# A transformer pair in one core: matrix products issued in four column strips behind the attention outputs, a new clock for transfers, and a newly searched order

## The chip, the core and the metric

The kernel runs on one core of a Trainium2 chip. The metric is the device time of one execution in microseconds. Before the change the median of three runs is 1472.46 us (1472.16 to 1474.3).

## What is computed

Two transformer blocks in sequence on `x` of shape (32, 128, 256), all in float32, with 16 heads of 16 and a hidden layer of 1024. Each block has self-attention, cross-attention to `ctx_1024`, and a feed-forward part. Cut to what matters:

```
# block 1; mod = silu(cond) @ ada_w + ada_b, split into 6
xm1 = ln(x) * (1 + scale_sa) + shift_sa
x = x + gate_sa * (attn(xm1 @ qkv_w + qkv_b) @ sa_proj_w + sa_proj_b)
x = x + attn_masked(ln(x) @ q_w + q_b, ctx @ kv_w + kv_b) @ ca_proj_w + ca_proj_b
xm3 = ln(x) * (1 + scale_ff) + shift_ff
x = x + gate_ff * (gelu(xm3 @ fc1_w + fc1_b) @ fc2_w + fc2_b)
# block 2: the same shape with adaptive norms, rope on q and k, other weights, no gates
x = x + attn(rope(adaln1(x) @ qkv_w.T)) @ sa_out_w.T
x = x + attn(rope(adaln2(x) @ q_w.T), rope(ctx @ k_w.T), ctx @ v_w.T) @ ca_out_w.T
x = x + gelu(adaln3(x) @ ffn_w1.T + ffn_b1) @ ffn_w2.T + ffn_b2
```

## The kernel before, in words

The batch of 32 is cut into 16 groups of two sequences (256 tokens). Each group passes both blocks, so there are 32 group passes; eight streams of groups are under way at once, and their steps are interleaved so that every engine has work of some stream.

**The matrix engine's three ways of working.** A float32 matmul of the program shows as two records in the profile, each with its own weights load; a transpose shows as one.

- *Full*: the products of 128 x 128 weights with 256 moving columns (`rows_T` L604, `values` L616, `project` L844), the transposes of the normed tile (`transposed` L565) and of the score maxima (L754).
- *Rows*: the scores (L729). Four heads at a time use 32 of the 128 rows each, `scores` is one PSUM tile of four banks, and a batch needs two such groups of 16 matmuls: one to find the maxima, one with the maxima subtracted from the queries.
- *Columns*: the attention outputs (L775). Four heads at a time use 32 of the 128 columns each, 16 matmuls to a group, into the PSUM tile `small`.

There are 128 batches (32 passes, two attentions, two sequences), so 256 rows groups and 128 columns groups. Products go to three PSUM tiles of one bank, `products0` to `products2`.

**One attention and what follows it.** Scores; VectorE takes the maxima (L741); TensorE turns them (L754); VectorE subtracts them from the queries (L758, tile `qa`); scores again; ScalarE takes the exponential (L767); the outputs (L775), whose sums of exponentials come along as extra columns; ScalarE copies them (L781). Then `over_sums` (L786 to L810): a DMA gathers the sums (`few`, L793), another the outputs (L795), VectorE takes the reciprocal (L798), a DMA writes it to DRAM (`inv`, L801), two DMAs bring it back spread (L806), and VectorE multiplies (L809). Only then may `project` (L844) start, after which `normed_T` runs: statistics on VectorE (L540, L541), the power on GpSimd (L547), the normed tile (L553), and the transposes (L565).

**What sets the order.** The instructions of each engine stand in a fixed order that a planner writes when the program is built. Every step is a generator that yields when it can start, on which engine, which buffers it needs and a rank. `Clock` (L41) keeps a planned time for each engine and buffer; its costs are constants in the code (`use`, L57; `dma`, L70; `load`, L75). `Tasks.run` (L143) takes step after step, the one with the earliest planned start, and breaks near ties by rank. `ORDER` (L35) holds one number for each 40 us of planned time; it sets how far a later step may be preferred and shuffles the ranks. The clock knows that TensorE loses time when it goes from one way of working to another (`TURN`, L46), and it counts buffers: one `sc` (`scores`), one `at` (`small`), three `mm` (`products`). All DMAs are issued by SyncE, in the order planned. In `dma`, a transfer takes a fixed time from its issue, whatever else is under way.

**Weights.** Each weight tile is loaded twice, first for block 1, later for block 2. `Weight.used` (L216) counts uses; at the last one of block 1 it issues the reload at once, inside the product's own step (`second`, L266), and the planner reckons 3.0 us for each.

Of the kernel before, what the change touches and what calls it, by code (L numbers as in the profile page):

```python
# [17 lines left out]
P = 128  # L18
# [16 lines left out]
ORDER = (  # L35
    6622, 0, 91896, 0, 27754, 24892, 69964, 0, 30721, 66120, 0, 41605, 0, 69433, 0, 43084, 27437, 27178, 72830,
    16201, 38328, 98324, 37276, 0, 13032, 79752, 41486, 59529, 18013, 48897, 61204, 13263, 51033, 0, 0, 0, 0
)


class Clock:  # L41
# [71 lines left out]
def when(t):  # L113
    return t() if callable(t) else t
# [93 lines left out]
class Weight:  # L208
# [6 lines left out]

    def used(self):  # L216
        self.left -= 1
        if self.left == 0:
            self.there[1] = self.load()


@with_exitstack
def two_blocks(ctx: ExitStack, tc: tile.TileContext, a: dict, out: bass.AP):
# [24 lines left out]
    p_a = pool("p_a", 1)  # L248
    p_s = pool("p_s", NS + 2)

    def mm(shape):
# [356 lines left out]

    def values(wm, hd, w, col, src, t):

        yield after(wm, w, t), "pe", "mm", 1.5
        slot = clock.take("mm")
        ps = mms[slot].rearrange("p (b d) -> p b d", d=D)
        for b in range(GB):
            for k in range(KC):
                nc.tensor.matmul(ps[:, b, :], lhsT=src[:, k, b * S:(b + 1) * S],  # L616
                                 rhs=w.t[:, k, col:col + D], start=(k == 0), stop=(k == KC - 1))
        w.used()
        t = clock.use("pe", 1.72)
        there = Event()  # L620

        def evict():
            yield t, "act", "", 2
            nc.scalar.copy(hd.v[:, :, :, 0], ps)  # L624
            clock.give("mm", slot, there.add(clock.use("act", 0.6)))

        tasks.spawn(evict(), wm)
        return there


    def paired(hd, wm, w, src, t):
# [30 lines left out]
        def move():  # L662
            yield here, "sp", "", 1
            nc.sync.dma_start(out=hd.k[0:P:2, :, :], in_=st[1:P:2, :, :])
            clock.give("st", at, there.add(clock.dma(2.7)))

# [25 lines left out]
    def turned(to, wm, w, col, src, t):  # L692
# [7 lines left out]
        def move():  # L700
            yield t, "dve", "", 1
            for b in range(GB):
                one = slice(b * S, (b + 1) * S)
                nc.vector.tensor_tensor(st[:, :, :, one], ps[:, :, one].unsqueeze(2).to_broadcast([P, 2, 2, S]), rope,  # L704
                                        ALU.mult)
            end = clock.use("dve", 1.25)
            clock.give("mm", slot, end)
            yield end, "pool", "", 1
            nc.gpsimd.tensor_tensor(st[:, 0], st[:, 0], st[:, 1], ALU.add)  # L709
            yield clock.use("pool", 1.27), "sp", "", 4  # L710
            for e in range(2):
                nc.sync.dma_start(out=to[2 * e:P:4, :, :], in_=st[:, 0, e, :])
                end = clock.dma(2.3)
            clock.give("st", at, there.add(end))
# [4 lines left out]
    def attention(wm, hd, masked, t, t_v, name, done):  # L719
# [13 lines left out]
        def batch(b):  # L733
# [14 lines left out]
            clock.give("sc", slot, t_top)  # L748
            yield (lambda: max(t_top, when(second[b - 1]) if b else 0.0)), "pe", "at qa" if ou else "at qa ou", 0.5
            at, less = clock.take("at"), clock.take("qa")  # L750
            if not ou:
                ou.append(clock.take("ou"))
            ps = ats[at][:, 0:S]
            nc.tensor.transpose(ps, top.rearrange("p r i -> p (r i)"), ident)  # L754
# [4 lines left out]
            end = clock.use("dve", 0.7)  # L759
            clock.give("at", at, end)  # L760
            yield end, "pe", "sc pt", 0
# [7 lines left out]
            clock.give("sc", slot, end)  # L769
            yield (lambda: max(end, when(t_v))), "pe", "at", 1  # L770
            at = clock.take("at")
            for c in range(C):
                for r in range(R):
                    i = (R * c + r) * HD
                    nc.tensor.matmul(ats[at][32 * r:32 * r + 32, c * S:(c + 1) * S],  # L775
                                     lhsT=v[:, b, i:i + HD, :].rearrange("p d t -> p (d t)"),
# [3 lines left out]
            yield end, "act", "", 1  # L780
            nc.scalar.copy(ous[ou[0]][:, :, cut], ats[at].rearrange("p (c s) -> p c s", s=S))  # L781
            end = clock.use("act", 0.6)
            clock.give("at", at, end)
            copied.add(end)

        def over_sums():  # L786
# [6 lines left out]
            nc.sync.dma_start(out=few, in_=o[1:P:8, :, :])  # L793
            at = clock.dma(2.1)
            nc.sync.dma_start(out=wm.xt, in_=o[0:P:2, :, :])  # L795
# [5 lines left out]
            nc.sync.dma_start(out=inv.rearrange("r (t w) -> (r t) w", w=w), in_=few)  # L801
            yield clock.dma(1.6), "sp", "", 1
            by = o[:, 0:KC, :]
            for c in range(2):
                half = inv[:, c * KC * GT:(c + 1) * KC * GT]
                nc.sync.dma_start(out=by[c:P:2, :, :], in_=half.unsqueeze(1).to_broadcast([n, 4, KC * GT]))  # L806
                at = clock.dma(2.5)
            yield at, "dve", "", 1.5
# [10 lines left out]
    def project(wm, x, lhs, n, w, ready, bias, gate, name):  # L819
# [18 lines left out]
        for b in range(GB):  # L838
# [4 lines left out]
            for k in range(n):  # L843
                nc.tensor.matmul(ps[:, b, :], lhsT=lhs(k, b), rhs=w.t[:, k, :], start=(k == 0), stop=(k == n - 1))  # L844
            t = clock.use("pe", 0.43 * n)
        w.used()
        yield t, "dve", "", 1
# [40 lines left out]
    def load_gate(wm, which, g):  # L888
# [3 lines left out]
        nc.sync.dma_start(out=t, in_=gates[which][g * GB:(g + 1) * GB, :].partition_broadcast(P))  # L892
        clock.dma(3.6)
        return y

    def mask_row(hd, src, g):
        yield landed("masks"), "sp", "", 1
        row = src.rearrange("b s -> (b s)")[g * GT:(g + 1) * GT].unsqueeze(0).unsqueeze(0)
        nc.sync.dma_start(out=hd.k[MASK:P:32, :, :], in_=row.to_broadcast([R, C, GT]))
        return clock.dma(2.5)  # L900

    class Context:
# [5 lines left out]
        def fetch(self, wm):  # L908
# [3 lines left out]
            load_ctx(self.slot, self.g)  # L912
            self.there.add(clock.dma(3.0))

# [68 lines left out]
    def stream(wm, mine, loaded):  # L983

        while loaded:
# [13 lines left out]
            def next_x(i):  # L999
                load_x(xs[i], a["x"] if then < NG else middle, then % NG)  # L1000
                return xs[i], clock.dma(2.9)

# [11 lines left out]
            nc.sync.dma_start(out=to[g * GB:(g + 1) * GB].rearrange("b s d -> s b d"), in_=x)  # L1014
            end = clock.dma(2.2)
            if first:
# [99 lines left out]
```

## Time and profile before

| | |
|---|---|
| median of the runs | 1472.46 us (1472.16 to 1474.3) |
| time of the profiled execution | 1467.35 us |
| its span, first to last instruction | 1465.5 us |
| TensorE busy (matmul) | 1433.2 us, 98% |
| TensorE weights loads | 1183.2 us, 81% |
| VectorE, ScalarE, GpSimd busy | 883.9, 700.6, 356.3 us (60%, 48%, 24%) |
| main DMA queue | 117.98 MB, 25.8% of 16 engines' span |
| granted TensorE clock, mean | 0.997 |

The profile is of one execution. The busy time of the matmul row is the union of records that overlap, with ends that are modelled, so it cannot be read as work done at full rate; the distance from one record's start to the next one's start can. The profiled execution took 5.1 us less than the median of the runs (1472.46 - 1467.35).

### The profile page before, as it was taken

What the parts mean: (1) busy time and instruction counts of PE and PEld (TensorE: products, weight loads), DVE (VectorE), ACT (ScalarE), POOL (GpSimd) and SP (SyncE); (2) the same over time, 40 slices, a digit from 0 to 9 for tenths busy, and PEclk for the clock granted to TensorE, in tenths of its full rate; (3) what the DMA queues carried; (4) which work ended last, traced back from release to release, by engine and by line L of the source; (5) the groups of instructions that cost most, each with busy time, mean ns of one, the idle gap of its engine ahead of it and who ended that gap; (6) DMA issues with size and microseconds to landing.
All of it is one profiled execution on the core that took longest, in us unless ns stands there. A gap on an engine that the chain in (4) does not pass through costs nothing.

```text
span 1465.5 us, 39524 instructions
## 1 busy us (share of the span) xinstructions
PE 1433.2 (98%) x17016; PEld 1183.2 (81%) x17016; DVE 883.9 (60%) x1546; ACT 700.6 (48%) x1120; POOL 356.3 (24%) x498
## 2 busy tenths in 40 slices
PE   8999999999999999999999999999999999999998
PEld 7887888887788778888887888888787888787887
DVE  6766545546564475457575676675866655865642
ACT  6444554464554545535534444444444444544452
POOL 3222223222232312332232221220222211211211
PEclk9999999999999999999999999999999999999999
DMA  6343221313223223323212331221313111221210
GB/s 228 117 128 88 83 73 50 88 63 116 71 65 86 79 89 84 90 86 121 82 49 91 114 125 46 85 66 50 111 57 104 41 55 59 76 78 56 69 48 22
DMA packets 107360, 120.52 MB, mean 82 GB/s; under 512 B 11632, under 2 KB 82992, under 8 KB 107184
## 3 DMA queue, kind: packets, MB, share of 16 engines
q1 hardware_dynamic: 107184, 117.98, 25.8%
q8 instruction: 134, 2.20, 0.6%
q14 instruction: 42, 0.34, 0.1%
HBM read 54.92 MB, written 12.68 MB: 46 GB/s over the span
## 4 chain that ended last, share of the span: by engine, by line
PE 75%; DMA 8%; DVE 8%; issue 3%; POOL 2%; SPq 2%; ACT 2%; DVEq 0%; ACTq 0%; POOLq 0%
PE products L604 24%; PE products L844 20%; PE scores L729 15%; PE small L775 7%; PE products L616 5%; PE products L565 3%; DVE top L741 2%; DMA ou<-inv_d 1%; PE small L754 1%; DMA inv_d<-few_d 1%; DMA few_d<-ou 1%; DVE st L704 1%; ACT exp L767 1%; SPq L806 1%; DMA ou<-inv_a 1%
## 5 line engine op out<-in xcount | busy, mean ns | idle before, releaser
L741 DVE TENSOR_REDUCE top<-scores 128x8 f32<-128x1024 f32 x256 | 300.2, 1214 | 59.7 <-PE scores L729 44.4
L767 ACT ACTIVATE exp<-scores 128x1024 f32<-128x1024 f32 x256 | 248.3, 1023 | 174.4 <-PE scores L729 173.4
L604 PE MATMUL products<-xt,w_ffn_w 128*128 128x256 f32 x1024 | 238.5, 384 | 0.3 <-ACT ht L873 0.2
L844 PE MATMUL products<-w_ffn_w,ht 128*128 128x256 f32 x1024 | 231.9, 381 | 0.0
L604 PEld LDWEIGHTS products<-xt,w_ffn_w 128*128 128x128 f32 x1024 | 189.3, 190 | 31.3 <-issue 1.8
L844 PEld LDWEIGHTS products<-w_ffn_w,ht 128*128 128x128 f32 x1024 | 191.8, 190 | 27.5 <-issue 0.8
L781 ACT COPY ou<-small 128x512 f32<-128x512 f32 x128 | 75.5, 590 | 210.5 <-PE small L775 209.9
L873 ACT ACTIVATE ht<-products,cols 128x256 f32<-128x256 f32 x256 | 116.4, 473 | 116.9 <-PE products L604 115.4
L729 PEld LDWEIGHTS scores<-qa,keys 32*128 32x128 f32 x4096 | 126.6, 187 | 44.7 <-issue 22.7
L709 POOL TENSOR_TENSOR st<-st 128x512 f32<-128x512 f32 x64 | 82.4, 1288 | 301.6 <-DVE st L704 295.3
L729 PEld LDWEIGHTS scores<-keys,queries 32*128 32x128 f32 x4096 | 126.0, 186 | 36.4 <-issue 21.2
L729 PE MATMUL scores<-qa,keys 32*128 32x128 f32 x4096 | 151.0, 284 | 3.4 <-DVE top L741 2.7
L729 PE MATMUL scores<-keys,queries 32*128 32x128 f32 x4096 | 150.4, 283 | 3.9 <-DVE top L741 1.8
L775 PE MATMUL small<-exp,values 128*32 128x128 f32 x4096 | 139.1, 276 | 0.1
L604 PE MATMUL products<-xt,w_qkv_w 128*128 128x256 f32 x512 | 125.0, 389 | 0.8 <-DVE xt L585 0.8
L775 PEld LDWEIGHTS small<-exp,values 128*32 128x32 f32 x4096 | 104.3, 109 | 24.2 <-issue 11.6
L758 DVE TENSOR_TENSOR qa<-queries,small 128x512 f32<-128x512 f32 x128 | 86.3, 674 | 55.7 <-PE small L754 50.9
L849 DVE TENSOR_TENSOR x<-products,x 128x512 f32<-128x512 f32 x64 | 43.9, 686 | 121.2 <-PE products L844 103.2
L604 PEld LDWEIGHTS products<-xt,w_qkv_w 128*128 128x128 f32 x512 | 94.3, 192 | 16.6 <-issue 2.4
L624 ACT COPY values<-products 128x512 f32<-128x512 f32 x64 | 40.0, 626 | 122.1 <-PE products L616 120.0
L809 DVE TENSOR_TENSOR xt<-xt,ou 128x512 f32<-128x512 f32 x64 | 48.2, 754 | 81.5 <-DMA ou<-inv_b 26.2
L704 DVE TENSOR_TENSOR st<-products,rope 128x512 f32<-128x512 f32 x128 | 81.8, 680 | 21.8 <-PE products L604 14.8
(111 smaller groups left out, 1734.5 us busy)
## 6 DMA issues: line engine op xcount, KB each, us to landing
xt<-ou SPq DMA_DIRECT2D x64, 256.0 KB
keys<-st SPq DMA_DIRECT2D x96, 128.0 KB
queries<-st SPq DMA_DIRECT2D x96, 128.0 KB
cxt<-in_ctx SPq DMA_DIRECT2D x32, 256.0 KB
x<-in_x SPq DMA_DIRECT2D x16, 256.0 KB
keys<-st SPq DMA_DIRECT2D x16, 256.0 KB
y<-gate_dram_sa SPq DMA_DIRECT2D x16, 256.0 KB
ou<-inv_a SPq DMA_DIRECT2D x32, 128.0 KB
```

Source lines behind the costliest of these rows:

```text
L604: nc.tensor.matmul(ps[:, c, :], lhsT=w.t[:, k, at:at + P], rhs=src[:, k, :], start=(k == 0), stop=(k == KC - 1))
L616: nc.tensor.matmul(ps[:, b, :], lhsT=src[:, k, b * S:(b + 1) * S], rhs=w.t[:, k, col:col + D], start=(k == 0), stop=(k == KC - 1))
L704: nc.vector.tensor_tensor(st[:, :, :, one], ps[:, :, one].unsqueeze(2).to_broadcast([P, 2, 2, S]), rope, ALU.mult)
L709: nc.gpsimd.tensor_tensor(st[:, 0], st[:, 0], st[:, 1], ALU.add)
L729: nc.tensor.matmul(sc[:, r, c * S:(c + 1) * S], lhsT=lhs(slice(32 * r, 32 * r + 32), c), rhs=rhs(slice(32 * r, 32 * r + 32), c), start=Tru ...
L741: nc.vector.tensor_reduce(top[:, r:r + 2, TOP:TOP + 2 * C:2], scs[slot][:, r:r + 2, :].rearrange("p r (c s) -> p r c s", s=S), AX.X, ALU.max)
L758: nc.vector.tensor_tensor(qa, q[:, :, cut], ps.unsqueeze(1).to_broadcast([P, C, S]), ALU.subtract)
L767: nc.scalar.activation(exps[pt][r // 2], scs[slot][:, r:r + 2, :], AF.Exp, scale=SCALE)
L775: nc.tensor.matmul(ats[at][32 * r:32 * r + 32, c * S:(c + 1) * S], lhsT=v[:, b, i:i + HD, :].rearrange("p d t -> p (d t)"), rhs=exps[pt][r ...
L781: nc.scalar.copy(ous[ou[0]][:, :, cut], ats[at].rearrange("p (c s) -> p c s", s=S))
L844: nc.tensor.matmul(ps[:, b, :], lhsT=lhs(k, b), rhs=w.t[:, k, :], start=(k == 0), stop=(k == n - 1))
L873: nc.scalar.activation(ht[f // (FC // 2)][:, f % (FC // 2), :], ps[:, 0, :], AF.Gelu, bias=b1[:, f:f + 1])
```

## The change

Five things are edited; the kernel's mathematics and tiles stay, apart from PSUM.

1. **Products behind outputs in columns.** A new function `multiply` issues a product either as one matmul of 128 weight columns or, if the planned way of working is "columns" at that point, as four matmuls of 32 weight columns, each to its own 32 partitions of the same PSUM tile. `rows_T`, `values` and `project` call it, and tell the clock that they take "any" way: columns if the engine is in columns, full otherwise.
2. **PSUM.** The tile `small` is gone, a fourth `products` tile takes its bank, and the turned maxima and the attention outputs take a `products` tile.
3. **The clock of transfers.** In `dma` a transfer's planned end comes behind that of the transfer before it (`moved`); the durations given to it are lowered by 0.1 to 0.5 us (one stays), the reloads' aside.
4. **Reloads.** A weight's reload is a step of its own on SyncE with rank 3, planned for the end of the last use. The two halves of the key and value weights are two steps. Their planned time depends on the size.
5. **Order.** `ORDER` holds new numbers, so that every engine's sequence is another one.

The diff, cut to its core:

```diff
 ORDER = (
-    6622, 0, 91896, 0, 27754, 24892, ...
+    71372, 36752, 0, 0, 71454, 91697, ...
 )
-        many = {"sc": 1, "at": 1, "mm": 3, "pt": 2, "set": NA, "qa": 2, "ou": 3, "st": 2, "ht": 1,
+        many = {"sc": 1, "mm": 4, "pt": 2, "set": NA, "qa": 2, "ou": 3, "st": 2, "ht": 1,
                 "y": 3, "cx": 3, "x": NS + 1}
+        self.moved = 0.0
...
         if engine == "pe":
+            if way == "any":
+                way = "columns" if self.way == "columns" else "full"
             took = took * self.PACE + (self.TURN[self.way] if way != self.way else 0.0)
             self.way = way
...
     def dma(self, took):
         start = max(self.now, self.free["sp"])
         self.free["sp"] = start + 0.64
-        return start + took
+        self.moved = max(self.moved, start + 0.9) + max(0.1, took - 1.4)
+        return self.moved + 0.5
 
     def load(self, kb):
...
         self.landed = max(self.landed, start + 1.5) + kb / 200.0
+        self.moved = self.landed
         return self.landed + 0.7
...
-    def used(self):
+    def used(self, at):
         self.left -= 1
         if self.left == 0:
-            self.there[1] = self.load()
+            self.load(self, at)
...
-    ats = [psum.tile([P, C * S], F32, name="small")]
-    mms = [psum.tile([P, 2 * GT], F32, name=f"products{i}") for i in range(3)]
+    mms = [psum.tile([P, 2 * GT], F32, name=f"products{i}") for i in range(4)]
...
+    def multiply(to, lhs, rhs, start=True, stop=True):
+        if clock.way == "columns":
+            for j in range(0, P, 32):
+                nc.tensor.matmul(to[j:j + 32], lhsT=lhs[:, j:j + 32], rhs=rhs, start=start, stop=stop)
+        else:
+            nc.tensor.matmul(to, lhsT=lhs, rhs=rhs, start=start, stop=stop)
...
-        def second():
-            n = cols // len(names)
-            for i, name in enumerate(names):
-                load(t[:, :, i * n:(i + 1) * n], f"L1_xcond_{name}")
-                end = clock.dma(3.0)
-            return end
+        def second(w, at):
+            def loading():
+                n = cols // len(names)
+                for i, name in enumerate(names):
+                    yield at, "sp", "", 3
+                    load(t[:, :, i * n:(i + 1) * n], f"L1_xcond_{name}")
+                    w.there[1] = clock.dma(2.0 + 3e-6 * 4 * rows * n)
+                    if i < len(names) - 1:
+                        w.there[1] = NEVER
+            tasks.spawn(loading(), Setup())
...
-                nc.tensor.matmul(ps[:, c, :], lhsT=w.t[:, k, at:at + P], rhs=src[:, k, :],
-                                 start=(k == 0), stop=(k == KC - 1))
-        w.used()
-        return slot, ps, clock.use("pe", 0.86 * n)
+                multiply(ps[:, c, :], w.t[:, k, at:at + P], src[:, k, :], k == 0, k == KC - 1)
+        end = clock.use("pe", 0.86 * n, "any")
+        w.used(end)
+        return slot, ps, end
...
-            yield (lambda: max(end, when(t_v))), "pe", "at", 1
-            at = clock.take("at")
+            yield (lambda: max(end, when(t_v))), "pe", "mm", 1
+            at = clock.take("mm")
```

More of the change, by code (lines that the diff above doesn't have):

```diff
@@ L35 @@
 ORDER = (
[L36 to L37 removed]
+    71372, 36752, 0, 0, 71454, 91697, 0, 94157, 73524, 26634, 81926, 67541, 0, 14443, 0, 59342, 0, 88828, 0,
+    12337, 30536, 2421, 29624, 8901, 84470, 22357, 96881, 43920, 51881, 25816, 98785, 9044, 8412, 0, 96954, 9117,
+    0
 )
@@ L615, in values @@
             for k in range(KC):
[L616 to L619, printed above, removed]
+                multiply(ps[:, b, :], src[:, k, b * S:(b + 1) * S], w.t[:, k, col:col + D], k == 0, k == KC - 1)
+        t = clock.use("pe", 1.72, "any")
+        w.used(t)
         there = Event()
@@ L664, in move @@
             nc.sync.dma_start(out=hd.k[0:P:2, :, :], in_=st[1:P:2, :, :])
-            clock.give("st", at, there.add(clock.dma(2.7)))
+            clock.give("st", at, there.add(clock.dma(2.3)))
         tasks.spawn(move(), wm)
@@ L712, in move @@
                 nc.sync.dma_start(out=to[2 * e:P:4, :, :], in_=st[:, 0, e, :])
-                end = clock.dma(2.3)
+                end = clock.dma(2.0)
             clock.give("st", at, there.add(end))
@@ L748, in batch @@
             clock.give("sc", slot, t_top)
-            yield (lambda: max(t_top, when(second[b - 1]) if b else 0.0)), "pe", "at qa" if ou else "at qa ou", 0.5
-            at, less = clock.take("at"), clock.take("qa")
+            yield (lambda: max(t_top, when(second[b - 1]) if b else 0.0)), "pe", "mm qa" if ou else "mm qa ou", 0.5
+            at, less = clock.take("mm"), clock.take("qa")
             if not ou:
                 ou.append(clock.take("ou"))
-            ps = ats[at][:, 0:S]
+            ps = mms[at][:, 0:S]
             nc.tensor.transpose(ps, top.rearrange("p r i -> p (r i)"), ident)
@@ L759, in batch @@
             end = clock.use("dve", 0.7)
-            clock.give("at", at, end)
+            clock.give("mm", at, end)
             yield end, "pe", "sc pt", 0
@@ L774, in batch @@
                     i = (R * c + r) * HD
-                    nc.tensor.matmul(ats[at][32 * r:32 * r + 32, c * S:(c + 1) * S],
+                    nc.tensor.matmul(mms[at][32 * r:32 * r + 32, c * S:(c + 1) * S],
                                      lhsT=v[:, b, i:i + HD, :].rearrange("p d t -> p (d t)"),
@@ L780, in batch @@
             yield end, "act", "", 1
-            nc.scalar.copy(ous[ou[0]][:, :, cut], ats[at].rearrange("p (c s) -> p c s", s=S))
+            nc.scalar.copy(ous[ou[0]][:, :, cut], mms[at].rearrange("p (c s) -> p c s", s=S))
             end = clock.use("act", 0.6)
-            clock.give("at", at, end)
+            clock.give("mm", at, end)
             copied.add(end)
@@ L793, in over_sums @@
             nc.sync.dma_start(out=few, in_=o[1:P:8, :, :])
-            at = clock.dma(2.1)
+            at = clock.dma(2.0)
             nc.sync.dma_start(out=wm.xt, in_=o[0:P:2, :, :])
@@ L801, in over_sums @@
             nc.sync.dma_start(out=inv.rearrange("r (t w) -> (r t) w", w=w), in_=few)
-            yield clock.dma(1.6), "sp", "", 1
+            yield clock.dma(1.5), "sp", "", 1
             by = o[:, 0:KC, :]
@@ L806, in over_sums @@
                 nc.sync.dma_start(out=by[c:P:2, :, :], in_=half.unsqueeze(1).to_broadcast([n, 4, KC * GT]))
-                at = clock.dma(2.5)
+                at = clock.dma(2.3)
             yield at, "dve", "", 1.5
@@ L843, in project @@
             for k in range(n):
-                nc.tensor.matmul(ps[:, b, :], lhsT=lhs(k, b), rhs=w.t[:, k, :], start=(k == 0), stop=(k == n - 1))
-            t = clock.use("pe", 0.43 * n)
-        w.used()
+                multiply(ps[:, b, :], lhs(k, b), w.t[:, k, :], k == 0, k == n - 1)
+            t = clock.use("pe", 0.43 * n, "any")
+        w.used(t)
         yield t, "dve", "", 1
@@ L892, in load_gate @@
         nc.sync.dma_start(out=t, in_=gates[which][g * GB:(g + 1) * GB, :].partition_broadcast(P))
-        clock.dma(3.6)
+        clock.dma(3.4)
         return y
@@ L899, in mask_row @@
         nc.sync.dma_start(out=hd.k[MASK:P:32, :, :], in_=row.to_broadcast([R, C, GT]))
-        return clock.dma(2.5)
+        return clock.dma(2.0)
     class Context:
@@ L912, in fetch @@
             load_ctx(self.slot, self.g)
-            self.there.add(clock.dma(3.0))
+            self.there.add(clock.dma(2.8))
     def attended(wm, at, x, masked, t, t_v, w, bias, gate, eps, mod, g, name, then, cx=None):
@@ L1000, in next_x @@
                 load_x(xs[i], a["x"] if then < NG else middle, then % NG)
-                return xs[i], clock.dma(2.9)
+                return xs[i], clock.dma(2.7)
             if then is not None and clock.slot("x") < NEVER:
@@ L1014, in stream @@
             nc.sync.dma_start(out=to[g * GB:(g + 1) * GB].rearrange("b s d -> s b d"), in_=x)
-            end = clock.dma(2.2)
+            end = clock.dma(2.1)
             if first:
```

## The prediction

> **What bounds the kernel now.** I read the page's busy shares first, then the chain that ended last, then TensorE's own waits, then a stretch of its timeline.
>
> ```profile
> span 1465.5 us, 39524 instructions
> ...
> PE 1433.2 (98%) x17016; PEld 1183.2 (81%) x17016; DVE 883.9 (60%) x1546; ACT 700.6 (48%) x1120; POOL 356.3 (24%) x498
> ...
> PE 75%; DMA 8%; DVE 8%; issue 3%; POOL 2%; SPq 2%; ACT 2%; DVEq 0%; ACTq 0%; POOLq 0%
> ```
>
> TensorE is the bound; no other engine passes 60%. A quarter of the chain runs over others, but eight streams fill those times, as TensorE's own waits show (us in total, times, longest):
>
> ```profile
> PE products L565 <- DVE y L553: 8.0, 7, 3.3
> PE products L844 <- DVE xt L809: 5.9, 8, 1.3
> PE scores L729 <- DVE top L741: 4.6, 7, 1.8
> ...
> PE scores L729 <- DMA keys<-st: 1.2, 1, 1.2
> ```
>
> All waits in that list sum to 27 us. So either TensorE's own work gets shorter, or little happens. How long the work is, the timeline of TensorE tells, read from start to start (ends overlap):
>
> ```profile
> 737.79 1.08 PE L775 MATMUL small<-exp,values 128*32 128x128 f32 x32
> 738.80 3.72 PE L844 MATMUL products<-w_ffn_w,ht 128*128 128x256 f32 x16
> 742.45 1.08 PE L775 MATMUL small<-exp,values 128*32 128x128 f32 x32
> 743.46 1.17 PE L729 MATMUL scores<-keys,queries 32*128 32x128 f32 x32
> 744.57 0.66 PE L565 MATMUL products<-ident,y 128*128 128x128 f32 x4
> 745.06 3.62 PE L844 MATMUL products<-w_ffn_w,ht 128*128 128x256 f32 x16
> 748.51 0.27 PE L754 MATMUL small<-ident,top 128*128 128x128 f32 x1
> 748.72 1.17 PE L729 MATMUL scores<-keys,queries 32*128 32x128 f32 x32
> ```
>
> Sixteen product records that stay among full ones take 748.51 - 745.06 = 3.45 us, 0.216 each. The same sixteen between two columns groups take 742.45 - 738.80 = 3.65: 0.2 us more for two changes of the way of working. Over all records, the medians of start-to-start times give the prices: leaving full costs 0.093 us (0.309 against 0.216); entering full costs 0.104 with a product first (its first record takes 0.320) and 0.056 with a transpose first (0.165 against 0.109). A columns group takes 1.01 us, eight rounds of 0.109 and 0.139 for coming and going. A rows group takes 1.104.
>
> **The change, part by part.** Products in columns, and the new order around them, are one sum. I counted the stretches of one way of working in the instruction order of both programs:
>
> - stretches in full: 272 before (180 begin with a product, 88 with a transpose, 4 with a small modulation), 238 after (111, 124, 3);
> - stretches in columns: 129 before, 115 after, of which 72 hold products besides outputs;
> - stretches in rows: 256 in both, so they cancel.
>
> Leaving full: 34 fewer x 0.093 = 3.2 us. Entering full: 69 fewer with a product x 0.104 = 7.2, 36 more with a transpose x 0.056 = 2.0, net 5.2. Columns: 14 fewer x 0.139 = 1.9. Sum **10.3 us**, all on TensorE, hence on the path. As a check, the same prices and every record of the order sum to 1411.1 us before and 1400.9 after; 1465.5 - 1411.1 = 54.4 us of the span before are then true waits, start and tail.
>
> The price of a product in columns: 458 of 2048 products become four matmuls each (the order has 1832 of 32 columns by 256), 916 rounds counting both records. No row before shows four column strips with 256 moving columns. The nearest are the outputs' rows (count, busy us and mean ns of one, idle):
>
> ```profile
> L775 PEld LDWEIGHTS small<-exp,values 128*32 128x32 f32 x4096 | 104.3, 109 | 24.2 <-issue 11.6 <-ACT exp L767 1.1 <-ACT ou L781 0.7
> L775 PE MATMUL small<-exp,values 128*32 128x128 f32 x4096 | 139.1, 276 | 0.1
> ```
>
> A weights load is 0.109 us, yet four loads and four matmuls of 128 columns pass in each 0.109: the loads lie fully beside the streaming. The Trainium skill speaks against this (TensorE: Matmul & The Clock Gate, "The mechanism"): a weights load overlaps a running matmul only when it goes to other rows of the array. Strips of columns share all rows, so by the rule every round would wait 0.109 for its loads: 916 x 0.109 = +100 us. By the row (and by the full products, which load for 0.190 beside 0.216 of streaming) nothing waits: 256 moving columns give twice the cover of 128 and the round takes the same 0.216 as a full matmul: 0 us. I take 0. Below nothing isn't possible, since the streaming rate is the same. If a little of the cover is lost, the nearest number is what a columns group pays on its first round beyond the later ones, 0.024 us: x 916 = 22 us. Both passes of an output add to the same place in PSUM, round after round, without a gap, so accumulating over k shouldn't cost either.
>
> The fourth product tile in place of `small`: TensorE's weights loads waited 3.6 and 0.7 us in all for the copies out of `small` (L781), and a shared pool can shorten that or spread it to products; I take 0, bounds -4 to +4. The steps on VectorE and ScalarE that read it are the same in number and size; one more pair of table loads on ScalarE (65 to 67, 1.28 us each) lies in an engine at 48%.
>
> The reloads: eight DMAs, at nearly the same places of SyncE's queue (246th to 369th row before, 241st to 367th after). Before, SyncE stood 3.0 us before a reload for the product that last used the tile, with the attention's sums and keys queued behind; TensorE waited for no weights. Gain 0 to 3, and if one is late, a megabyte at the page's early 228 GB/s is about 5 us once. I take 0.
>
> The clock of transfers moves no transfer by itself; it leaves more room before the steps that wait for one. In the chain the same step takes from 1.98 to 3.28 us (`few`) and 2.53 to 3.55 (`ou` from `inv`), where the old clock has 2.1 and 2.5. What room can win is bounded by what TensorE waits behind DMAs: 5.9 us at L844 for the multiply of L809, about 4.6 more at its weights loads, 1.2 for keys: up to 12 us.
>
> Against it stands the new order, which is tighter elsewhere. Between two uses of the one `scores` tile, the exponential needs some 2.4 us (two of 1.02 and the hops). In PE work at the prices above, the old order leaves less in 8 places, 2.0 us short in all; the new one in 11 places, 7.9 us short (four of them in the first 110 us). From project to transposes the shortest gaps are 4.0, 4.0 and 4.2 us against 4.7, 4.8 and 4.7. Together some +8 us of new waits against up to -12 of removed ones. I let them cancel: the 54.4 us stay.
>
> Sum: span 1465.5 - 10.3 = 1455.2, profiled execution 1457; the median of the runs lies 5.1 above, **1462.2 us** (-0.7%).
>
> **Rivals.**
> - *The waits shrink* (chance 0.20). The 12 us behind DMAs go and the tight places cost little because they fall together with waits that stand there anyway: 1462.2 - 12 = 1450. For it: the spread of the transfers' times. Against: TensorE waits longest for VectorE, which no clock of transfers mends.
> - *Column products are slower* (0.12), the case on the other side. One mechanism: in the 72 mixed stretches each round pays part of its four loads. At 0.024 us a round it is 1462.2 + 22 = **1484**; by the skill's rule 1562. It decides from 10.3/916 = 0.011 us a round. Against it: the outputs' rounds of 0.109 without loss.
> - *The waits grow* (0.20): the tight places cost their 8 us, again as much behind them as other streams come late, and nothing is won at the DMAs: 1462.2 + 16 = 1478; half of that gives 1470.
> - *The change doesn't do what it says*: the order of the changed program shows the strips and the fewer stretches, so only their price is open; no chance of its own.
>
> **How the numbers follow.** The forecast's case has 0.48. Within 0.2% (1469.5 to 1475.4, about what a measurement of this kernel can tell from no change) lies half of the growing waits. Faster: 0.48 + 0.20 + 0.04 (the mildest growth) = 0.72. Same: 0.11. Slower: 0.12 + 0.05 = 0.17. The range reaches from 1448, just past the shrinking waits, to 1477 for most of the growing ones; the dear strips are left out. The likeliest case's own range is 1456 to 1469.
>
> **What would show it.** Right: sixteen product records of 32 columns by 256 between two columns groups follow at 0.216 a round, four records a round; no 0.32 first record after an output; TensorE's records sum to about 1401 and the rest of the span stays near 54. Wrong if the mean round of the strips is above 0.227, or if that rest moves by over 10 us; then the waits at `scores`, L565 and the multiply ahead of project tell which.

## The result, and the profile after

The changed kernel takes **1463.71 us** (median of 6 runs, 1459.99 to 1465.63) against 1472.95 us for the kernel before beside it (6 runs, 1472.16 to 1474.3): a ratio of 0.9934, 95% interval 0.9918 to 0.995. The forecast was 1462.2. The profiled execution took 1462.32 us, 1.4 us below the median; its mean granted TensorE clock was 0.994, where before's was 0.997.

The page of the kernel after, its span, its busy row and the shares of the chain:

```profile
span 1460.5 us, 45118 instructions
...
PE 1425.4 (98%) x19764; PEld 1136.3 (78%) x19764; DVE 889.2 (61%) x1538; ACT 707.5 (48%) x1130; POOL 357.2 (24%) x498
...
PE 83%; DVE 6%; DMA 5%; ACT 2%; POOL 2%; issue 1%; SPq 1%; DVEq 0%; ACTq 0%; POOLq 0%
```

There are 2748 more matmul records and 7.8 us less matmul busy time: the records have become smaller, and the stretches fewer. TensorE's share of the chain has gone from 75% to 83%, the transfers' from 8% to 5%.

The timeline of TensorE in the kernel after (start, duration, line, operation, output and inputs, tile, count) shows what a product in columns costs:

```profile
429.86 3.64 PE L262 MATMUL products<-w_ffn_w,ht 128*32 128x256 f32 x64
433.43 1.17 PE L749 MATMUL scores<-qa,keys 32*128 32x128 f32 x32
434.53 3.72 PE L264 MATMUL products<-w_ffn_w,ht 128*128 128x256 f32 x16
438.09 0.27 PE L774 MATMUL products<-ident,top 128*128 128x128 f32 x1
...
748.05 1.08 PE L795 MATMUL products<-exp,values 128*32 128x128 f32 x32
748.95 1.91 PE L262 MATMUL products<-w_qkv_w,xt 128*32 128x256 f32 x32
750.79 1.17 PE L749 MATMUL scores<-qa,keys 32*128 32x128 f32 x32
```

Thirty-two strips are eight rounds of four. From the strips' first start to the scores behind them they take 750.79 - 748.95 = 1.84 us: eight rounds of 0.216 and the 0.11 that leaving the columns costs anyway. The sixteen rounds at 429.86 take 3.57, again 0.216 each. The outputs ahead of them take 748.95 - 748.05 = 0.90 instead of 1.01, because the engine stays in columns. The sixteen full records at 434.53 behind a scores group take 3.56: sixteen of 0.216 and 0.104 for entering full. So a round of strips costs what a full record costs, although its four loads share all rows of the array with the matmul that runs. The rule of the Trainium skill that the prediction weighed (TensorE: Matmul & The Clock Gate, "The mechanism") does not hold here as it was read; by it, as an estimate, the 1.84 us would have been 8 x (0.216 + 0.109) + 0.11, about 2.7. The same section of the Trainium skill also lets a load go ahead into a background weight buffer; that would fit, but no run here shows how the loads are hidden.

What remains are TensorE's waits. The list for the kernel after (engine, line, the one waited for: us in total, times, longest):

```profile
PE products L586 <- DVE y L574: 6.7, 10, 2.4
PE scores L749 <- ACT exp L787: 6.7, 9, 1.8
PE products L264 <- DVE xt L829: 3.7, 6, 1.7
PE products L774 <- DVE top L766: 3.4, 2, 2.9
PE scores L749 <- DVE top L761: 2.7, 4, 1.0
PE products L262 <- DVE xt L829: 2.2, 2, 1.8
```

The line L829 (L809 before) multiplies the outputs by the inverted sums, which come back by a chain of small transfers. TensorE's waits for it were 5.9 us before and 3.7 + 2.2 = 5.9 after. A clock meant to leave more room for transfers won nothing there. The waits for the last step of the maxima (L766, from 1.6 us) and for the exponential (L787, from 0.4) have grown.

To tell work from waits I split every start-to-start time of TensorE into two parts: what the record and its change of way cost at the prices of the prediction, and the excess. The excess is the time that TensorE lost to waits and, where the granted clock was below 1, to slower working. About 6 us of each span lie at its start and tail. This trace count is some 6 us above the prediction's count from the instruction order in each kernel, which drops out of differences.

| kernel | span | records and changes of way | excess | of it in stretches at half clock |
|---|---|---|---|---|
| before | 1465.5 | 1416.8 | 42.6 | 4.9 |
| after | 1460.5 | 1407.5 | 47.1 | 8.2 |
| new order, full products (first experiment) | 1454.9 | 1418.5 | 30.5 | 3.1 |

The records have become shorter by 9.3 us (10.3 predicted). In these traces the excess grew by 4.5. But each trace is one execution, and that of before was 5.6 us faster than the median of its runs (1472.95 - 1467.35), that of after 1.4. By the medians the gain is 9.2 us, as much as the records got shorter, so the growth lies within what single executions differ by. The third row is the surprise that the experiments had to explain.

### The profile page after: what moved, and what is told of

It is laid out like the page before. It is cut to its first block, busy times and chain, and to the rows that moved or that the text cites. A ratio compares the mean times of both kernels' runs of the same rounds, so it can differ in the third digit from the quotient of the medians.

```text
span 1460.5 us, 45118 instructions
## 1 busy us (share of the span) xinstructions
PE 1425.4 (98%) x19764; PEld 1136.3 (78%) x19764; DVE 889.2 (61%) x1538; ACT 707.5 (48%) x1130; POOL 357.2 (24%) x498
## 4 chain that ended last, share of the span: by engine, by line
PE 83%; DVE 6%; DMA 5%; ACT 2%; POOL 2%; issue 1%; SPq 1%; DVEq 0%; ACTq 0%; POOLq 0%
PE products L264 42%; PE scores L749 16%; PE products L262 11%; PE products L795 7%; PE products L586 3%; DVE top L761 2%; PE products L774 1%; DMA y<-gate_dram_sa 1%; ACT exp L787 1%; DVE y L574 1%; DMA ou<-inv_e 1%; DVE st L724 1%; DVE xt L829 1%; DMA ou<-inv_a 1%; PE products L475 1%
## 5 line engine op out<-in xcount | busy, mean ns | idle before, releaser
L787 ACT ACTIVATE exp<-scores 128x1024 f32<-128x1024 f32 x256 | 248.3, 1023 | 168.3 <-PE scores L749 157.6
L264 PE MATMUL products<-w_ffn_w,ht 128*128 128x256 f32 x848 | 193.4, 382 | 0.0
L264 PE MATMUL products<-xt,w_ffn_w 128*128 128x256 f32 x760 | 176.7, 383 | 0.4 <-DVE x L869 0.4
L264 PEld LDWEIGHTS products<-w_ffn_w,ht 128*128 128x128 f32 x848 | 158.5, 190 | 23.1
L264 PEld LDWEIGHTS products<-xt,w_ffn_w 128*128 128x128 f32 x760 | 140.8, 190 | 22.2 <-DVE x L869 0.8
L801 ACT COPY ou<-products 128x512 f32<-128x512 f32 x128 | 75.5, 591 | 166.7 <-PE products L795 157.9
L795 PE MATMUL products<-exp,values 128*32 128x128 f32 x4096 | 139.0, 278 | 0.0
L778 DVE TENSOR_TENSOR qa<-queries,products 128x512 f32<-128x512 f32 x128 | 86.1, 675 | 66.3 <-PE products L774 65.7
L795 PEld LDWEIGHTS products<-exp,values 128*32 128x32 f32 x4096 | 106.7, 110 | 22.8 <-issue 11.1
L829 DVE TENSOR_TENSOR xt<-xt,ou 128x512 f32<-128x512 f32 x64 | 49.3, 770 | 87.3 <-DMA ou<-inv_d 29.8
L264 PE MATMUL products<-xt,w_qkv_w 128*128 128x256 f32 x336 | 83.2, 394 | 0.8 <-DVE xt L606 0.8
L877 POOL TENSOR_TENSOR x<-y,x 128x512 f32<-128x512 f32 x32 | 40.8, 1276 | 164.1 <-DVE y L873 164.0
```

Source lines behind the costliest of these rows:

```text
L264: nc.tensor.matmul(to, lhsT=lhs, rhs=rhs, start=start, stop=stop)
L778: nc.vector.tensor_tensor(qa, q[:, :, cut], ps.unsqueeze(1).to_broadcast([P, C, S]), ALU.subtract)
L787: nc.scalar.activation(exps[pt][r // 2], scs[slot][:, r:r + 2, :], AF.Exp, scale=SCALE)
L795: nc.tensor.matmul(mms[at][32 * r:32 * r + 32, c * S:(c + 1) * S], lhsT=v[:, b, i:i + HD, :].rearrange("p d t -> p (d t)"), rhs=exps[pt][r ...
L801: nc.scalar.copy(ous[ou[0]][:, :, cut], mms[at].rearrange("p (c s) -> p c s", s=S))
L829: nc.vector.tensor_tensor(wm.xt, wm.xt, by, ALU.mult)
```

## The experiments

Theory A says that the gain is the strips'. Theory B says that it is the new order's, whose waits are shorter. Later a theory F was added: both would gain, but a shorter TensorE stretch turns into waits, because some transfers come back after a time of their own, however short the work is that covers them. Ratios are to runs of the kernel before on the same chip.

### Full products in the new order

```diff
     def multiply(to, lhs, rhs, start=True, stop=True):
-        if clock.way == "columns":
+        if False:
```

> The changed kernel with its planner and order untouched, but every product issued as one full matmul. Counted by the same prices, its stretches of one way of working rise (full 238 to 285, of them beginning with a product 111 to 185; columns 115 to 125) and TensorE's records sum to 1412.7 us instead of 1400.7, 12.0 us more. Theory A (the strips bring the gain, at no price of their own): about 1463.7 + 12 = 1475.7, at or above the kernel before. Theory B (the gain comes from the new order and the new clock of transfers, the strips only shift changes of way about): within 4 us of the changed kernel, 1460 to 1468.

Measured: 1458.34 us (1456.72 to 1462.12), ratio 0.993 (0.9916 to 0.9944). Counted from the order, its TensorE work is 12.0 us longer than after's (1412.7 against 1400.7), and it is not slower than after (0.9934). Theory A falls here. The page's chain and TensorE's longest waits in this kernel:

```profile
PE 89%; DVE 5%; DMA 2%; POOL 1%; ACT 1%; issue 1%; SPq 0%; DVEq 0%; ACTq 0%; POOLq 0%
```

```profile
PE scores L749 <- ACT exp L787: 6.2, 8, 1.8
PE products L586 <- DVE y L574: 4.6, 8, 1.5
PE products L264 <- DVE xt L829: 2.7, 4, 1.2
```

More of the chain runs over TensorE (89%), and the waits behind the returned sums are 2.7 us instead of 5.9. The excess is 30.5 us: against before, the change without its strips takes 12.1 us of excess away while the records stay about as long as they were (+1.7). The ratio of the medians agrees: 0.7% of 1472 is 10.3 us, and the records are 1.7 longer. TensorE's listed waits fell by 7.8 of these 12.1 us (26.7 to 18.9): those for the maxima from 7.9 to 1.3, for the transposes' input (`y`) from 8.0 to 4.6, for the multiply from 5.9 to 2.7, while those for the exponential rose from 0.4 to 6.2.

### Strips in the old order

The kernel before, with strips wherever products follow outputs directly. Its planner is not told, so its order is the old one.

```diff
+    way = ["full"]
+
+    def multiply(to, lhs, rhs, start=True, stop=True):
+        if way[0] == "columns":
+            for j in range(0, P, 32):
+                nc.tensor.matmul(to[j:j + 32], lhsT=lhs[:, j:j + 32], rhs=rhs, start=start, stop=stop)
...
+            way[0] = "columns"
```

> The kernel before with its planner, its PSUM tiles and its order untouched; products that stand behind outputs are issued as four strips of 32 columns (382 of 2048 products). By the counted prices TensorE's records fall from 1411.0 to 1400.1 us, 10.9 less. Theory A: about 1472.9 - 10.9 = 1462, as fast as the whole change or a little faster, since the old order's waits and its half-clock windows (three of 3.4 us) stay. Theory B: the old order's time within 4 us, 1469 to 1473.

Measured: 1461.92 us (1460.51 to 1466.35), ratio 0.9952 (0.9938 to 0.9967). The count of its stretches gave 10.9 us less; about 7 came (0.0048 of 1470). So strips are worth something in the old order. Theory B alone is not the answer either: each of the two edits gains about 0.5 to 0.7% alone, and both together gain 0.7%. Why strips keep most of their gain in the old order and none in the new one was not tested.

### Waits filled with idle matmuls

The granted clock fell to half in three stretches of the kernel after. This kernel puts 20 products of the identity with itself into four waits, so that TensorE is not idle there.

```diff
+FILL = {13: 4, 16: 2, 17: 8, 241: 6}
...
         def group_rows(sc, lhs, rhs):
+            n = FILL.get(groups[0], 0)
...
+                for _ in range(n):
+                    nc.tensor.matmul(mms[i][:, 0:P], lhsT=ident, rhs=ident, start=True, stop=True)
```

> The changed kernel, order untouched, with 20 idle-filling matmuls of the identity into a free product tile at four places where TensorE waits ahead of scores (at 88.5, 102.3, 104.3 and 1321 us; 4, 2, 8 and 6 of 0.218 us each). They compute nothing that is used. Theory C (the 10 us of half clock that begin at 105.6 and at 1324.1 come from those waits): both half-clock stretches vanish, the waits themselves stay as long as they were, and the time falls by about 4 to 5 us, to 1459. Theory D (the half clock has another cause, or comes at its own times): the stretches stay and the time is unchanged or up to 1 us longer.

Measured: 1459.02 us (1456.81 to 1461.92), ratio 0.9934 (0.9919 to 0.9949). The half clock at 105.6 and at 1324.1 us was gone, a new stretch stood at 590.5, and that at the start stayed. The ratio is that of the change, so this one alone decides nothing on the time. On the half clock it shows less than it seems to: a second profile of the change itself, without filling (below), has none at 1324 us either, but has that at 106.2 us again. So only the place at 105.6 speaks for filling.

### Without the transfers that come back

Both versions, without the softmax sums' way (gather, reciprocal, out to memory, back) and without the gates' loads.

```diff
-            nc.sync.dma_start(out=few, in_=o[1:P:8, :, :])
...
-            nc.vector.reciprocal(few, few)
...
-            nc.sync.dma_start(out=inv.rearrange("r (t w) -> (r t) w", w=w), in_=few)
...
-                nc.sync.dma_start(out=by[c:P:2, :, :], in_=half.unsqueeze(1).to_broadcast([n, 4, KC * GT]))
...
-        nc.sync.dma_start(out=t, in_=gates[which][g * GB:(g + 1) * GB, :].partition_broadcast(P))
```

> The changed kernel with its order, but without the transfers that come back late: the attention's sums aren't gathered, inverted and spread (no `few`, no reciprocal, no `inv`, no way back), the multiply of the outputs takes unnormalized values instead, and the gates aren't loaded. So its output isn't the reference's. It goes with e6, which is the same with full products. Theory F (the strips' 11 us are lost because other engines' chains that hang on those transfers end the waits, so that less TensorE work only means more waiting): with the transfers gone, the strips gain again, e5 8 to 12 us shorter than e6. Theory G (the strips have a cost of their own that the records don't show, or the chains that bind don't hang on transfers): e5 within 3 us of e6. Both expect e5 below the changed kernel, near 1435 to 1450.

> As e5, the same transfers left out (its output isn't the reference's either), with every product full as in e1. Theory F: 8 to 12 us longer than e5. Theory G: within 3 us of e5.

Measured: with strips 1437.84 us (1436.66 to 1439.65), ratio 0.976 (0.9741 to 0.9778); with full products 1448.35 us (1447.62 to 1453.17), ratio 0.9837 (0.9814 to 0.986). The strips are worth 10.5 us here, the count of the prediction, and the intervals are apart. The table of excess says the same:

| | with returns | without | cost of the returns |
|---|---|---|---|
| strips (after) | 47.1 | 24.4 | 22.7 |
| full products | 30.5 | 22.1 | 8.4 |

The returns cost the strips' version 14.3 us more than the full one in these traces (11.9 by the ratios: 0.9934 - 0.976 against 0.993 - 0.9837), at least the 11.0 by which its records are shorter. So the strips have no hidden cost of their own, and what takes their gain away hangs on what was left out. That is what theory F says, with one reservation: the edit leaves out more than transfers. SyncE has fewer to issue, and VectorE loses 64 reciprocals (its busy time falls from 889.2 to 842.1 us with strips, from 886.3 to 841.9 with full products). The time of the transfers was not parted from these.

### Which of the transfers

> The changed kernel with its order; of the transfers that come back late only those of the attention's sums are left out (no `few`, reciprocal, `inv` and its way back; the outputs are multiplied by unnormalized values, so its output isn't the reference's). e5, which leaves out the gates' loads too, was 2.4% below the kernel before. If the sums' round trip is what ends the waits: within 4 us of e5's 0.976. If the gates' loads: near the changed kernel's 0.993. If both bind in turn: about half way, 0.982 to 0.988.

> The changed kernel with its order; only the loads of the gates are left out (the gate tiles hold what was there before, so its output isn't the reference's). If the gates' loads end the waits: near 0.977. If the sums' round trip: near 0.992. If both bind in turn: 0.982 to 0.988.

The edits are the first four and the last removed line above, each alone in the strips' version. Without the sums' way: 1439.92 us (1439.51 to 1442.57), ratio 0.9772 (0.9745 to 0.9799). Without the gates' loads: 1453.15 us (1451.16 to 1453.53), ratio 0.9854 (0.9831 to 0.9876). Against the change beside them (0.9919, below) they gain 0.0147 and 0.0065, both together 0.0159 (on another chip). So the two overlap, and the sums' way is the main one. In the run without the gates' loads VectorE's work stays (895.7 us), so there it is the transfers or their place in SyncE's queue. Both runs have strips alone; how much of the strips' own 11 us each of the two takes is not shown. The first groups of TensorE's waits without the sums' way:

```profile
PE scores L749 <- ACT exp L787: 5.6, 10, 1.4
PE products L586 <- DVE y L574: 4.5, 8, 1.0
```

The waits behind L829 are nearly gone (0.6 us), as they must be. Those at the transposes (L586) fell from 6.7 to 4.5, but a second profile of the change has 4.0 there, so this fall is within the spread. How long VectorE stands at L829, its own waits say, after and in the full version (the two longest groups of each):

```profile
DVE xt L829 <- DMA ou<-inv_d: 29.8, 11, 5.2
DVE xt L829 <- DMA ou<-inv_b: 24.5, 12, 5.3
```

```profile
DVE xt L829 <- DMA ou<-inv_b: 22.1, 11, 4.8
DVE xt L829 <- DMA ou<-inv_d: 16.6, 8, 3.4
```

Over all streams VectorE waits 84 us for these returns in the kernel after, 56 in the full version, 71.5 before. The list overstates the difference: it puts 10.9 us at the same multiply in the full version down to ScalarE. All idle time of VectorE ahead of these multiplies is 87, 73 and 81.5 us. Part of that was idle time anyway; what stands behind it on VectorE is not. The way of the sums, from the issue of the gather to the multiply, takes 11.7 us in the mean after (8.7 to 21.3), 11.5 in the full version, 10.6 before. It does not shrink when TensorE's work does.

One place shows a chain of this kind whole, with the gates' load. The chain of waits after, with start and duration, and then of the full version at the same step:

```profile
579.04 4.44 DMA y<-gate_dram_sa
...
583.54 0.75 POOL gb_a L854
...
586.60 1.25 POOL x L877
...
587.87 0.44 DVE st_b L561
...
588.95 2.35 DVE top L761 x2
...
591.65 0.30 PE products L774
```

```profile
577.47 3.71 DMA y<-gate_dram_sa
...
585.55 0.44 DVE st_b L561
...
589.33 0.30 PE products L774
```

The timelines of TensorE there (the bracket is the idle time before, and what ended it):

```profile
585.10 1.91 PE L262 MATMUL products<-xt,w_q_w 128*32 128x256 f32 x32
586.83 1.91 PE L262 MATMUL products<-w_k_w,cxt 128*32 128x256 f32 x32
591.65 0.30 PE L774 MATMUL products<-ident,top 128*128 128x128 f32 x1 [2.91 <-DVE top L766]
```

```profile
586.57 1.89 PE L264 MATMUL products<-w_k_w,cxt 128*128 128x256 f32 x8
589.33 0.30 PE L774 MATMUL products<-ident,top 128*128 128x128 f32 x1 [0.87 <-DVE top L766]
```

The gate's load starts 1.6 us later and takes 0.7 longer after than in the full version; GpSimd and VectorE behind it work equally long. TensorE's own work, in strips, ends about as early as in full, and it waits 2.0 us longer. The wait is put down to VectorE (`top`), which had itself stood for GpSimd, which had stood for the transfer. Why the load starts later, the queue of SyncE says, after and then in the full version:

```profile
572.89 1.19 SPq L826 DMA_DIRECT2D ou<-inv_a  x2
579.04 1.03 SPq L912 DMA_DIRECT2D y<-gate_dram_sa  x1
```

```profile
571.22 1.28 SPq L826 DMA_DIRECT2D ou<-inv_a  x2
577.47 0.45 SPq L912 DMA_DIRECT2D y<-gate_dram_sa  x1
```

SyncE issues in a fixed order. It stood 1.9 us for the write of the inverted sums (`inv_a`), 0.5 in the full version, and everything behind it, the gate's load too, comes 1.6 to 1.7 us later. So here the return was slow, and the strips did not make TensorE early. The other half of theory F, that early work only waits longer, shows at the same step with full products and a filled start (the last experiment), while without the gates' loads TensorE does not wait there:

```profile
584.79 1.89 PE L279 MATMUL products<-w_k_w,cxt 128*128 128x256 f32 x8
589.23 0.45 PE L797 MATMUL products<-ident,top 128*128 128x128 f32 x1 [2.55 <-DVE top L787]
```

```profile
583.65 1.91 PE L262 MATMUL products<-w_k_w,cxt 128*32 128x256 f32 x32
585.50 0.33 PE L774 MATMUL products<-ident,top 128*128 128x128 f32 x1
```

With the filled start TensorE comes 1.8 us earlier than in the full version without it (584.79 against 586.57), waits 2.55 us instead of 0.87, and goes on at 589.23 instead of 589.33: the gate's load starts at 577.46 and 577.47. This is one place; that the other waits arise in the same manner is what the runs without transfers support, not something traced for each.

### Old numbers in the new planner

```diff
 ORDER = (
-    71372, 36752, 0, 0, 71454, 91697, ...
+    6622, 0, 91896, 0, 27754, 24892, ...
 )
```

> The changed kernel with the order's numbers of the kernel before, which were not searched for this planner. TensorE's records sum to 1400.4 us by the prices, like the changed kernel's 1400.7. If the search of the numbers brought the shorter waits, its waits are longer by 10 us or more, 1472 to 1485. If they come from the clock of transfers and the shared product tiles, it is within 5 us of the changed kernel.

> As e7, and transfers are planned with the old clock: each ends a fixed time after its issue, with the old durations. Records sum 1401.4 us. If planning transfers one behind the other shortens the waits by itself, e8 is 5 to 15 us longer than e7, and its waits behind DMAs are longer; if not, the two are within 5 us or the sign is the other.

The second kernel also has the old clock of transfers and their old durations. Measured: 1539.42 us (1533.7 to 1543.44), ratio 1.0446 (1.0409 to 1.0483); and 1522.08 us (1518.29 to 1525.88), ratio 1.033 (1.03 to 1.0361). The records of the first sum to 1407.2 us, as after's; the excess is 124.0. The first is far above what was expected of it. So the numbers of the order are worth some 75 us (1539.4 - 1463.7), all of it excess, and these numbers, found for one planner, are bad ones for the other. The new clock doesn't shorten this unsearched order, it is 17 us longer with it. Each is one draw, so what the clock is worth after a search of its own stays open.

### More filling, and the change again

Beside e3's places, 13 idle products ahead of the turned maxima at 588 us, and 8 in the start.

```diff
-FILL = {13: 4, 16: 2, 17: 8, 241: 6}
+FILL = {13: 4, 16: 2, 17: 8, 241: 6, ("turn", 53): 13, ("tile", 0): 4, ("product", 0): 4}
```

> The changed kernel, order untouched, with 41 idle-filling matmuls of the identity: those of e3, 13 more ahead of the turn that waited 2.9 us at 588 us, and four each ahead of the first transposes and the first product, before which the half clock of the start begins. Theory C (a stretch of 3.4 us in which TensorE stood idle for about half is followed by half clock): one or no half-clock stretch but the start's, and the start's falls from 6.8 to 3.4 us; 3 to 5 us below the changed kernel in the same session (e12). Theory D: no difference from e12 beyond 1 us.

> The changed kernel once more, for the comparison with e9 on the same chip: ratio to the kernel before within its earlier interval, 0.992 to 0.995, with half-clock stretches that sum to 10 to 20 us of which half is lost.

Measured: 1456.75 us (1453.75 to 1462.63), ratio 0.9889 (0.9864 to 0.9914), the fastest complete kernel of the study; the change beside it 1462.99 us (1457.52 to 1464.57), ratio 0.9919 (0.9897 to 0.994). The intervals overlap slightly, so a gain of some 6 us is likely and not proved. The engines by windows (stretch, its length, busy time and count of TensorE's matmuls, its loads, VectorE, ScalarE and GpSimd, granted clock, DMA share, GB/s), after and then with the filling:

```profile
0.00:40.00 40.00, 37.01 (x261) 30.91 (x262) 27.36 (x80) 27.41 (x49) 12.47 (x32) 0.91 0.67 209
80.00:120.00 40.00, 36.54 (x562) 29.63 (x561) 25.62 (x40) 15.96 (x25) 11.79 (x16) 0.91 0.39 115
```

```profile
0.00:40.00 40.00, 38.21 (x290) 32.45 (x291) 29.60 (x87) 28.18 (x50) 13.47 (x34) 1.00 0.68 218
80.00:120.00 40.00, 39.64 (x643) 32.56 (x645) 27.68 (x44) 18.65 (x29) 11.94 (x16) 1.00 0.42 123
```

In both windows more gets done on TensorE, VectorE and ScalarE (TensorE has 29 and 81 records more, of which 16 and 28 are idle products), and TensorE's clock is 1.00 instead of 0.91. If the gain is real, 41 idle products (8.9 us of TensorE) cost less than they bring. This profile itself fell on one of the two longest runs (1462.62); it has half-clock stretches at 636.7, 769.8 and 855.1 us, where nothing is filled, against one or none expected. Its runs at a clock of 0.999 took 1455.56 and 1455.34.

### Full products with filling

```diff
+FILL = {13: 4, 16: 2, 17: 8, ("tile", 0): 4, ("product", 0): 4}
...
-        if clock.way == "columns":
+        if False:
```

> The changed kernel's planner and order, every product full as in e1, and the idle-filling matmuls of the first 110 us only (22 of them). Theory F (on this order the strips are worth nothing) with theory C (filled waits keep the clock up): the start's 6.8 us of half clock go, ratio to the kernel before 0.988 to 0.991, as e9 has it with strips. If the strips are worth a part of their 11 us once the clock stays up: 0.993 or above, slower than e9.

Measured: 1462.88 us (1459.76 to 1469.28), ratio 0.9938 (0.9915 to 0.996). The expectation was missed: with clocks of 0.997 to 1.000 it is no faster than without filling (0.993). Its excess is 29.3 us, and the fillers are 4.8 more of records. Beside the strips with filling (0.9889) the intervals just touch. What the strips are worth on the new order therefore stays between nothing (after against e1) and about 7 us (0.9938 - 0.9889 = 0.0049 of 1472, with filling, on different chips, and with two more places filled in the strips' kernel).

## Why the prediction was right, and where only by cancellation

- **TensorE bounds, and its records become shorter.** Right: 9.3 us in the trace against 10.3 counted. The prices of a change of way are those that the timeline after shows (0.90 for outputs that stay in columns, 3.56 for sixteen records that enter full).
- **A round of strips costs nothing more.** Right: 0.216 a round. The rival of dear column products, from 0.011 us a round, is out, and with it the rule as it was read for it.
- **"All on TensorE, hence on the path".** This step failed. The 10.3 us are on the path only while nothing else ends later. In the kernel with returns, the strips' 11.0 us came back as 16.6 us of excess in the traces (30.5 to 47.1), of which 5.1 lie in half-clock stretches; by the medians, where the strips' kernel and the full one are equal, as about 12. Without the returns they counted in full (10.5 us). Of the 16.6, only 3.2 are TensorE's own waits for the multiply (2.7 to 5.9), and 5.3 are waits for the maxima (1.3 to 6.6). I had measured how often TensorE waits for a transfer, but not how little slack the planned return of the sums has: it takes 10.6 to 11.7 us in the mean, under TensorE work that in its shortest places is about 9 us.
- **"The 54.4 us stay".** The total came out near: by the trace's count the rest of the span went from 1465.5 - 1416.8 = 48.7 to 1460.5 - 1407.5 = 53.0 us, so it moved by 4.3, within the 10 us that I gave. But it is a sum of two moves that I had together at zero: the change without its strips took 12.1 us away, and the strips gave 16.6 back in the traces, about 12 by the medians. In size that is the rival of shrinking waits and the rival of growing waits, both at once, and that they cancelled is luck. In mechanism neither was as named: only 3.2 of the 12.1 us were waits for the multiply with the returned sums, and the growth came with the returns.
- **Up to 12 us at the transfers against 8 us at tight places.** The transfers' part failed: the wait behind the multiply with the returned sums is 5.9 us before and after. The tight `scores` tile cost nearly what was feared: waits for the exponential went from 0.4 to 6.7 us. The idle time ahead of the second scores groups doubled, as these rows show (before, then after; the idle time stands behind the second bar):

```profile
L729 PE MATMUL scores<-qa,keys 32*128 32x128 f32 x4096 | 151.0, 284 | 3.4 <-DVE top L741 2.7 <-ACT xt L575 0.2
L749 PE MATMUL scores<-qa,keys 32*128 32x128 f32 x4096 | 151.1, 284 | 7.3 <-ACT exp L787 3.5 <-DVE top L761 2.7 <-DVE qa L778 1.0
```

- **The fourth product tile and the reloads at 0.** No wait for a product tile or a late weight is among TensorE's six longest groups. Neither was tried alone.
- **Left out: the granted clock.** The prediction priced every wait at its length. Before loses 4.9 us in half-clock stretches, after 8.2, so the change's waits were 3.3 us dearer than their length in these two traces.
- **From profile to median.** I carried over 5.1 us; it was 1.4. It made up for most of the 5.3 us by which the span was longer than forecast (1460.5 against 1455.2), so the 1.5 us between forecast and median flatter the working.

What stays open: whether the strips' gain is lost to the time of the returning transfers alone, or also to the VectorE and SyncE work that comes with them; the worth of the new clock of transfers with a search of its own, and how much of the 12.1 us of the new order is the clock's, the fourth tile's or the search's. They weren't told apart.

## What to carry to other kernels

Work that is taken off the busiest engine is gained only where no round trip with a length of its own has to end under it: before counting it as gain, compare each such round trip with the shortest work that covers it, and try the edit once with the round trips left out. When several edits come together, run each alone: here each had 0.5 to 0.7% alone and both had 0.7%. An order that was searched for one set of costs is not an order for another, so edit and search can be judged only together.

## What the runs showed of the hardware

- **Column strips run at full rate.** Four loads of 128 x 32 and four matmuls with 256 moving columns pass in 0.216 us, one full record's time, also while they add up over k in PSUM.
- **A short idle time halves the clock.** In the kernel after, TensorE waited 0.58 and 1.85 us within a few us, and then ran at half speed for 6.8 us. Its timeline:

```profile
102.91 1.17 PE L749 MATMUL scores<-qa,keys 32*128 32x128 f32 x32 [0.58 <-DVE top L761]
104.01 0.33 PE L774 MATMUL products<-ident,top 128*128 128x128 f32 x1
106.19 2.09 PE L749 MATMUL scores<-qa,keys 32*128 32x128 f32 x32 [1.85 <-ACT exp L787]
108.21 1.94 PE L795 MATMUL products<-exp,values 128*32 128x128 f32 x32
```

  The scores take 2.09 instead of 1.17 and the outputs 1.94 instead of 1.08. The stretches begin at 10.0, 105.6 and 1324.1 us; their distances are 28.0 and 357.0 times 3.413 us, and the trace gives each a length of 3.413 or 6.827 us. So the clock seems to be set in steps of 3.413 us, by how busy the step before was. I laid such steps from the first stretch over the traces of all 14 kernels, without the first 10 us, the end, and steps that are at half clock themselves. All 26 steps in which TensorE stood idle for 1.81 us or more were followed by half clock; of 13 between 1.59 and 1.80 us, 7 were; of 5844 below that, one. A wait of 2.9 us at 588.7 us in the kernel after was not followed by it: it lay over two steps, 1.5 us in the fuller one. The same wait can thus be free in one run and dear in another, by where the steps fall, which fits the spread of the runs (clocks of 0.991 took 1465.3 and 1465.6, of 0.996 took 1460.0).

- **The start has a half-clock stretch unless it is filled.** Each of the 12 kernels whose start is not filled has one of 3.4 or 6.8 us that begins between 8.4 and 11.6 us; the two whose start is filled have none.
